# Within-chunk sums of a linear-recurrence mixer: multiply-and-reduce on two vector engines, or coefficient blocks sent through DRAM to the matrix engine

## The chip, the cores and the metric

The kernel runs on one core of one Trainium2 chip. The core has a matrix engine (PE in the profile; PEld is its weight load), a vector engine (DVE), an activation engine (ACT), a general engine (POOL, called G in the code) and a queue that issues transfers (SP). Each engine takes its instructions in the order in which the program lists them. The metric is device time in microseconds, as the median of several runs; lower is better.

## The reference, cut to what matters

Eight batch elements of 256 tokens by 512 features pass through a transformer layer (self attention, cross attention, MLP) and then through a layer of the RWKV kind: a time mix, which is a recurrence over tokens with 32 heads of 16 features, and a channel mix. The change concerns the recurrence:

```python
def step(s, rkvw):
    r_t, k_t, v_t, w_t = rkvw
    a = k_t[..., :, None] * v_t[..., None, :]
    out = jnp.einsum('bhi,bhij->bhj', r_t, u * a + s)
    s = a + w_t[..., :, None] * s
    return (s, out)
```

For one head, `out_t` is the sum over earlier tokens s < t of a coefficient A[t, s] times v_s, where A[t, s] is the product of r_t, the decays between s and t, and k_s, summed over the 16 features; the token itself counts with u in place of the decay.

## The kernel before

All arithmetic is float32. Projections split each operand into a high and a low float32r part and use three matmuls (lines 185 to 187). The kernel is one program, cut into stages, one call per batch element. The first layer's stages come first; the second layer's are

- `a` (layernorm, token shift, low-rank mix), `b` (projections g, k) and `e` (projections v, w, r). r, k, v and w of each batch element are written to DRAM.
- `c`: tokens are cut into 16 chunks of 16. r, k and w come back from DRAM in tiles `in` with (8 head groups x 16 chunks) on the 128 partitions, so that a partition holds 16 tokens of 4 heads. POOL multiplies pairs of r and k (lines 713, 714, 724, 737), DVE reduces each product over 16 features into the coefficient tile `A` (715, 730, 743), and POOL multiplies decays into r, k and w in place, doubling the reach each round (747, 748, 749). Then, for t = 0 to 15, POOL multiplies the coefficients of token t by v of tokens 0 to t (755) and DVE sums over the source tokens (762) into `ob`. The decayed k and r, the chunk decays and `ob` are stored to DRAM (`ks`, `r0`, `dd`, `on`).
- `d`: the part that crosses chunks. Small matmuls of 32x32 (807) make the contribution of each chunk to the state, a scan on DVE runs over chunks (824), small matmuls (834) apply r to the states, and their masked sums are added to `o`, which was loaded from `on` (819). A normalisation ends it, and `o` goes to DRAM as `yg`.
- `f` and `g`: the channel mix, `front` and `back`.

The order of the work is decided at build time. `SEQ` lists in which order the stages are emitted, `AT` gives each stage a priority (1000 times batch index plus offset; lower goes first), and a scheduler then fixes the order of the instructions on each engine from these priorities and its own estimates. `SLOTS` names for each tile the buffers that it takes turns in; `BANKS` does so for PSUM. `wtp` is one bank, `up` two, and `staged` tiles take turns in two buffers.

`n_tile` loads 128 tokens by 512 features from a DRAM tile that is stored by head groups; `pm` is a mask over partitions: columns 2 and 3 are one where the partition's 16-token chunk within a pair is the even or the odd one.

Of the kernel before, what the change touches and what calls it, by code (L numbers as in the profile page):

```python
# [9 lines left out]
AF = mybir.ActivationFunctionType  # L10
ALU = mybir.AluOpType
AX = mybir.AxisListType
# [5 lines left out]
P = 128  # L18
D = 512
# [20 lines left out]
def slots(text):  # L40

    r = {}
    for item in text.split():
# [15 lines left out]
    "mlp": slots("w:a8-a11 x:a0,a1 xr:a2 y:a3 u:a4-a7 hf:a12,a13 hid:a16-a23 row:b8"),  # L59
    "time": slots(  # L60
        "w:a24,a25 x:a0 xs:a4-a7 y:a3 s:a8-a11 m2h:d0 m2g:a14,a15 n:b0,b1 d2:b9 m1:d1 xn:d2 xa:d3,a13 xb:d5 "
        "in:a16-a19 ob:a12 vm:a20,a21 r0t:a22 sts:a23 on_:a2 "
        "ks:b2,b3 X:a24,a25 A:a1 sq:b8 cm:c2 gr:c3 dts:c6 s0t:c7"
    ),
    "chan": slots(
# [3 lines left out]


SEQ = (
    "a0 b0 a1 e0 c0 b1 a2 e1 c1 d0 b2 a3 e2 c2 d1 b3 a4 e3 c3 d2 b4 a5 e4 c4 d3 b5 a6 e5 c5 d4 b6 a7 e6 c6 d5 b7 "
    "e7 c7 f0 d6 f1 g0 d7 f2 g1 f3 g2 f4 g3 f5 g4 f6 g5 f7 g6 g7"
)

BANKS = {
# [5 lines left out]

AT = {"a": -0.5, "b": -8.75, "e": 1.8, "c": -9.5, "d": -9.3, "f": 6.25, "g": 7.75}
PACE = 1000

def r32(ap):
# [4 lines left out]
def block_kernel(ctx: ExitStack, tc: tile.TileContext, a: dict, out: bass.AP):  # L93
    nc = tc.nc
# [34 lines left out]
    def wt(name, shape, dt=F32):  # L129
        tag = name  # L130
        if name in SLOTS[phase[0]]:
            tags = SLOTS[phase[0]][name]
            i = turn.get((phase[0], name), 0)
            turn[phase[0], name] = i + 1
            tag = tags[i % len(tags)]
        return wk.tile(shape, dt, name=name, tag=tag)
# [162 lines left out]
    def dtile(name, shape):  # L299
        return dram.tile(shape, F32, name=name)  # L300
# [235 lines left out]
    def staged(shape):  # L536
        return wst.tile(shape, F32, name="w")

    class TimeMix:
# [148 lines left out]
        def c(self, b, got):  # L688

            rd, kd, vd, wd = got  # L690

            def from_dram(src):
                d_ = wt("in", [P, 16, 64])
                nc.sync.dma_start(out=d_, in_=src.rearrange("e (c t) d -> (e c) t d", t=16))
                return d_

            kb, rb, wb = (from_dram(z) for z in (kd, rd, wd))

            vt = wt("in", [P, 64, 16])
            for h in range(2):  # L700
                vh = staged([P, 8, 64])
                nc.sync.dma_start(out=vh, in_=vd.rearrange("e (c t) d -> (e c) t d", t=16)[:, 8 * h : 8 * h + 8, :])
                S.copy(vt[:, :, 8 * h : 8 * h + 8].rearrange("p d s -> p s d"), vh)


            A = wt("A", [P, 16, 16, 4])

            def part(t, s_, dims):
                return bass.AP(A.tensor, A.offset + 64 * t + 4 * s_, [A.ap[0], *dims])

            X = wt("X", [P, 1024])
            X3 = X.rearrange("p (t d) -> p t d", t=16)
            G.tensor_tensor(X3, rb, kb, ALU.mult)
            G.tensor_tensor(X3, X3, W["ubc"].unsqueeze(1).broadcast_to([P, 16, 64]), ALU.mult)
            V.tensor_reduce(part(0, 0, [[68, 16], [1, 4]]), X.rearrange("p (t g i) -> p t g i", t=16, i=16), AX.X, ALU.add)


            for m in (1, 2, 4, 8):
                nb = 8 // m
                R, K, Wd = (z.rearrange("p (n u) d -> p n u d", n=nb) for z in (rb, kb, wb))  # L720
                if m < 4:
                    for i in range(m):
                        X = wt("X", [P, 1024])[:, 0:512]
                        G.tensor_tensor(
                            X.rearrange("p (n s d) -> p n s d", n=nb, s=m),
                            R[:, :, m + i : m + i + 1, :].broadcast_to([P, nb, m, 64]),
                            K[:, :, 0:m, :],
                            ALU.mult,
                        )
                        V.tensor_reduce(part(m + i, 0, [[136 * m, nb], [1, 4 * m]]), X.rearrange("p (n g i) -> p n g i", n=nb, i=16), AX.X, ALU.add)  # L730
                else:
                    ni = 16 // m
                    for n in range(nb):
                        for i in range(0, m, ni):
                            t0, s0 = (2 * n + 1) * m + i, 2 * n * m
                            X = wt("X", [P, 1024])
                            G.tensor_tensor(
                                X.rearrange("p (i s d) -> p i s d", i=ni, s=m),
                                rb[:, t0 : t0 + ni, :].unsqueeze(2).broadcast_to([P, ni, m, 64]),
                                kb[:, s0 : s0 + m, :].unsqueeze(1).broadcast_to([P, ni, m, 64]),  # L740
                                ALU.mult,
                            )
                            V.tensor_reduce(part(t0, s0, [[64, ni], [1, 4 * m]]), X.rearrange("p (n g i) -> p n g i", n=ni, i=16), AX.X, ALU.add)

                wl_ = Wd[:, :, m - 1 : m, :]
                wr_ = Wd[:, :, 2 * m - 1 : 2 * m, :]
                G.tensor_tensor(R[:, :, m:, :], R[:, :, m:, :], wl_.broadcast_to([P, nb, m, 64]), ALU.mult)
                G.tensor_tensor(K[:, :, :m, :], K[:, :, :m, :], wr_.broadcast_to([P, nb, m, 64]), ALU.mult)
                G.tensor_tensor(wr_, wr_, wl_, ALU.mult)

            ob = wt("ob", [P, 16, 64])
            for t in range(16):
                n = t + 1
                Y = wt("X", [P, 1024])[:, : 64 * n] if t else ob[:, 0, :]
                G.tensor_tensor(  # L755
                    Y.rearrange("p (h j s) -> p h j s", h=4, j=16),
                    A[:, t, 0:n, :].rearrange("p s h -> p h s").unsqueeze(2).broadcast_to([P, 4, 16, n]),
                    vt[:, :, 0:n].rearrange("p (h j) s -> p h j s", j=16),
                    ALU.mult,
                )  # L760
                if t:
                    V.tensor_reduce(ob[:, t, :], Y.rearrange("p (d s) -> p d s", s=n), AX.X, ALU.add)  # L762

            def back(src, name):
                dst = dtile(f"{name}_{b}", [8, T, 64])
                nc.sync.dma_start(out=dst.rearrange("e (c t) d -> (e c) t d", t=16), in_=src)
                return dst

            dd = dtile(f"dd_{b}", [8, 16, 64])
            nc.sync.dma_start(out=dd.rearrange("e c d -> (e c) d"), in_=wb[:, 15, :])  # L770
            return back(kb, "ks"), back(rb, "r0"), dd, vd, back(ob, "on")

        def d(self, b, got):

            ksd, r0d, dd, vd, ond = got
            dn = staged([16, D])
            nc.sync.dma_start(out=dn.rearrange("c (e d) -> c e d", e=8), in_=dd.rearrange("e c d -> c e d"))
            dt_ps = bank("wtp", [P, KC, 16])
# [8 lines left out]
            centred(s0t.rearrange("p g j -> p (g j)"), KC, bank("wtp", [P, KC]))  # L787
            ks = [self.n_tile(ksd, t, "ks") for t in range(2)]

            vms = []  # L790
            for t in range(2):
                vms.append(wt("vm", [P, 2, D]))
                vn = self.n_tile(vd, t)
                for par in range(2):
                    S.activation(vms[t][:, par, :], vn, AF.Copy, scale=pm[:, 2 + par : 3 + par])

            sts = wt("sts", [P, KC, 32, 16])
            for hp in range(2):
# [15 lines left out]
            r0 = [self.n_tile(r0d, t) for t in range(2)]  # L814
            r0t = wt("r0t", [P, KC, T])
            to_t(r0, lambda k2, tp: S.copy(r0t[:, 2 * k2 : 2 * k2 + 2, :], tp), "wtp")
            o = wt("on_", [P, 2, D])
            for t in range(2):
                nc.sync.dma_start(out=o[:, t, :].rearrange("p (e d) -> p e d", e=8), in_=ond[:, t * P : (t + 1) * P, :].rearrange("e p d -> p e d"))
            for g in range(KC):  # L820
                dT = bank("up", [P, 32, 16])
                S.copy(dT, dts[:, g, :].unsqueeze(1).broadcast_to([P, 32, 16]))
# [42 lines left out]
    class ChannelMix:  # L865
# [55 lines left out]
        def back(self, b, got):  # L921
            x4, xr, xk = got
            rr = [wt("rr", [P, D]) for t in range(2)]
            proj_n([W["fr"]], [xr], lambda t, o: S.activation(rr[t], o, AF.Tanh, scale=0.5), "o2")
            kh = wt("kk", [P, KC, T], F32R)
            kl = wt("kk", [P, KC, T], F32R)

            def emit3(ks, o):
                kf = wt("kf", [P, 2, T])
                S.activation(kf, o, AF.Relu)  # L930
                V.scalar_tensor_tensor(o, o, 0.0, kf, ALU.max, ALU.mult)
                S.copy(kh[:, ks, :], o)
                V.tensor_tensor(kl[:, ks, :], o, r32(kh[:, ks, :]), ALU.subtract)

            proj_t(W["fk"], xk, emit3, "o2", pairs=True)

            def emit4(t, o):
                V.scalar_tensor_tensor(o, rr[t], 1.0, o, ALU.add, ALU.mult)
                V.scalar_tensor_tensor(x4[:, t, :], o, 0.5, x4[:, t, :], ALU.mult, ALU.add)

            proj_n([W["fv"]], [(kh, kl)], emit4, "o2")
            nc.sync.dma_start(out=tok(out[b]), in_=x4)
# [4 lines left out]
    got = {}  # L947
# [80 lines left out]
```

## Time and profile before

| What | us |
|---|---|
| Median of 3 runs (1970.3 to 1984.28) | 1973.3 |
| The profiled execution: its span, and its time as a run | 1980.5, 1982.31 |
| PE busy | 1756.4 |
| DVE busy | 1379.7 |
| ACT busy | 1106.5 |
| POOL busy | 747.5 |
| First and last start of the product that opens `c` (713) | 1239.2, 1727.9 |
| First start of the first small matmuls of `d` (807), last start of the second ones (834) | 1322.8, 1819.0 |

Times within the span are counted from its start. A group of instructions is given by line, engine, operation and tile; the number behind x is how often it stands in the trace, then come the time in which any of them ran and the mean time of one. Matmuls overlap each other, so the mean time of one is more than the distance between two starts. The code's 1024 small matmuls of line 807 (128 for each of 8 batch elements) are 2048 records in the trace, and so are those of line 834.

### The profile page before, as it was taken

The page shows a single profiled execution, that of the slowest core. Times are in us where ns is not written, and L with a number is a line of the kernel's source. Part 1 is how long each engine was busy: PE and PEld are TensorE (multiplying, and loading weights), DVE is VectorE, ACT ScalarE, POOL GpSimd, SP SyncE. Part 2 cuts the span into 40 slices and gives each one's busy share as a digit, 9 for nine tenths or more (in the row PEclk, how much of TensorE's full clock was granted, in tenths as well). Part 3 has the DMA queues.
Part 4 walks back from the last instruction along what each step waited for, and adds up shares of the span by engine and source line. Part 5 has one row for each costly group of instructions (what it writes and reads, how often), then busy time and mean ns, then how long its engine had stood idle before and what let it go on. Part 6 is the DMA issues. An engine that isn't in the chain of part 4 may idle for free.

```text
span 1980.5 us, 38765 instructions
## 1 busy us (share of the span) xinstructions
PE 1756.4 (89%) x14576; PEld 1471.8 (74%) x14576; DVE 1379.7 (70%) x3211; ACT 1106.5 (56%) x2745; POOL 747.5 (38%) x550
## 2 busy tenths in 40 slices
PE   4999999989999998999999988888889895789877
PEld 4777777777777776799999976676777673677766
DVE  4777777776778687665654454669678788888554
ACT  3877777887778688532332334354464454355342
POOL 2111111121221221232311100898899999992000
PEclk9999999999999999999999998988898886888888
DMA  6644444656555556322311133454556476442210
GB/s 189 158 125 119 118 118 125 190 142 164 132 146 143 133 135 207 110 90 69 107 65 64 54 128 103 116 142 125 157 138 165 130 195 184 142 108 97 75 64 22
DMA packets 237170, 247.35 MB, mean 125 GB/s; under 512 B 156292, under 2 KB 159244, under 8 KB 236983
## 3 DMA queue, kind: packets, MB, share of 16 engines
q1 hardware_dynamic: 236982, 244.87, 44.7%
q8 instruction: 115, 1.88, 0.4%
q14 instruction: 73, 0.59, 0.1%
HBM read 118.71 MB, written 58.98 MB: 90 GB/s over the span
## 4 chain that ended last, share of the span: by engine, by line
PE 60%; DVE 15%; DMA 6%; ACT 6%; POOL 5%; issue 3%; SPq 3%; POOLq 0%; DVEq 0%; ACTq 0%
PE o L185 8%; PE o L186 8%; PE o L187 8%; PE mm L185 5%; PE mm L186 4%; PE mm L187 4%; PE tr L366 3%; PE out L187 3%; PE out L186 3%; PE out L185 3%; DVE e L359 3%; POOL X L755 2%; PE cx L375 2%; DVE e L357 2%; PE sc L355 2%
## 5 line engine op out<-in xcount | busy, mean ns | idle before, releaser
L362 ACT ACTIVATE e<-e,mx 128x256 f32<-128x256 f32 x512 | 256.7, 506 | 43.0 <-DVE mx L359 42.0
L357 DVE TENSOR_TENSOR e<-sc,mc 128x512 f32<-128x512 f32 x256 | 172.1, 683 | 111.8 <-PE sc L355 56.2
L227 POOL TENSOR_TENSOR u<-y,u 128x1024 fp32r<-128x1024 f32 x32 | 78.5, 2452 | 440.8 <-ACT u L226 440.6
L359 DVE CUSTOM_DVE_ANT_0 e<-e,mn 128x256 f32<-128x256 f32 x512 | 220.6, 473 | 1.0
L755 POOL TENSOR_TENSOR X<-A,in 128x128 f32<-128x128 f32 (+14 forms) x120 | 209.3, 1779 | 14.7 <-DVE ob L762 12.4
L185 PE MATMUL o<-whi,s 128*128 128x512 f32 x320 | 148.4, 464 | 49.4 <-ACT s L890 31.8
L366 PE MATMUL tr<-ident,e 128*128 128x128 f32 x1024 | 174.7, 285 | 18.0 <-ACT e L362 14.7
L185 PE MATMUL mm<-u,whi 128*128 128x256 f32 x512 | 153.7, 301 | 14.3 <-DVE s L319 7.8
L370 ACT COPY pt<-tr 128x512 f32<-128x512 f32 x256 | 147.0, 582 | 34.6 <-PE tr L366 33.9
L366 PEld LDWEIGHTS tr<-ident,e 128*128 128x128 f32 x1024 | 122.3, 144 | 49.2 <-ACT e L362 24.2
L186 PE MATMUL mm<-u,whi 128*128 128x256 f32 x512 | 147.5, 288 | 4.0 <-POOL u L227 4.0
L185 PE MATMUL o<-u,whi 128*128 128x256 f32 x512 | 144.7, 287 | 3.1 <-ACT whi L171 1.6
L187 PE MATMUL mm<-u,wlo 128*128 128x256 f32 x512 | 147.0, 287 | 0.0
L186 PE MATMUL o<-u,whi 128*128 128x256 f32 x512 | 144.0, 283 | 0.0
L187 PE MATMUL o<-u,wlo 128*128 128x256 f32 x512 | 144.0, 283 | 0.0
L186 PE MATMUL o<-wlo,s 128*128 128x512 f32 x320 | 141.4, 442 | 0.0
L293 POOL TENSOR_TENSOR xr<-xr,row 128x512 f32<-128x512 f32 x48 | 65.7, 1388 | 186.0 <-DMA xr<-in_x 81.1
L355 PE MATMUL sc<-stk 128*128 128x256 f32 x512 | 118.0, 322 | 19.3 <-DVE e L357 13.9
L187 PE MATMUL o<-whi,s 128*128 128x512 f32 x320 | 134.4, 438 | 0.6 <-DVE s L891 0.5
L507 ACT ACTIVATE hf<-o,cv 128x256 f32<-128x256 f32 x128 | 59.8, 475 | 117.8 <-PE o L187 115.0
L197 POOL TENSOR_SCALAR rstd<-mv 128x2 f32<-128x2 f32 x48 | 17.2, 357 | 281.2 <-DVE mv L195 260.5
L185 PEld LDWEIGHTS o<-whi,s 128*128 128x128 f32 x320 | 70.0, 219 | 68.8 <-ACT s L890 33.3
(324 smaller groups left out, 5296.3 us busy)
## 6 DMA issues: line engine op xcount, KB each, us to landing
stk<-s SPq DMA_DIRECT2D x512, 128.0 KB, 2.4
x<-x SPq DMA_DIRECT2D x40, 512.0 KB, 4.7
x<-xr SPq DMA_DIRECT2D x24, 512.0 KB, 3.6
xr<-x SPq DMA_DIRECT2D x16, 512.0 KB, 4.8
w<-in_w SPq DMA_DIRECT2D x16, 512.0 KB, 6.7
w<-v SPq DMA_DIRECT2D x32, 256.0 KB, 3.2
x<-in_x SPq DMA_DIRECT2D x8, 512.0 KB
xr<-in_x SPq DMA_DIRECT2D x8, 512.0 KB, 3.6
```

The source lines that it names most:

```text
L185: TE.matmul(o, ah, bh, start=first, stop=False)
L186: TE.matmul(o, ah, bl, start=False, stop=False)
L187: TE.matmul(o, al, bh, start=False, stop=last)
L227: (eng or V).tensor_tensor(lo, y, r32(hi), ALU.subtract)
L293: G.tensor_tensor(x[:, t, :], x[:, t, :], r, ALU.add)
L355: TE.matmul(sc[:, t, :], qs[hm][:, hc, t * P : (t + 1) * P], ks[hm][:, hc, :], start=True, stop=True)
L357: V.tensor_tensor(e, sc, mc, ALU.mult)
L359: V.tensor_tensor_reduce(e[:, t, :], e[:, t, :], mn[:, t, :], 1.0, 3.0e38, ALU.add, ALU.min, accum_out=mx[:, kk2, hc, t : t + 1])
L362: S.activation(pr[:, t, :], e[:, t, :], AF.Exp, bias=mx[:, kk2, hc, t : t + 1], scale=-1.0, accum_out=sums[:, kk2, hc, t : t + 1])
L366: TE.transpose(pt_ps[:, kk, t * P : (t + 1) * P], pr[:, t, kk * P : (kk + 1) * P], ident)
L370: S.copy(pt, pt_ps)
L755: G.tensor_tensor(Y.rearrange("p (h j s) -> p h j s", h=4, j=16), A[:, t, 0:n, :].rearrange("p s h -> p h s").unsqueeze(2).broadcast_to([P ...
```

## The change

The coefficient tile `A` is laid out by source token, head and target token, is made once and filled with zeros, so that coefficients with s > t stay zero. The products with v and their sums leave `c`: lines 755 and 762, the two loads of v with their transposing copies (702, 703), and the store and load of `on`. Instead `c` stores `A` to DRAM (`ad`). `d` loads it with the 128 source tokens of a half (8 chunks of 16) on the partitions (`At`), writes two masked copies into `Ax`, so that for each head a block of 32 source tokens by 32 target tokens is block diagonal (even and odd chunk), and multiplies each block by the 32 tokens' v of that head: 4 blocks for each of 32 heads and 2 halves. The sums stand in one `wtp` bank per half and are copied to `o`. In `SEQ`, `d` stands one `c` later, and its priority offset goes from -9.3 to 4.

```diff
-        "in:a16-a19 ob:a12 vm:a20,a21 r0t:a22 sts:a23 on_:a2 "
+        "in:a16-a18 At:a19 Ax:a12 vm:a20,a21 r0t:a22 sts:a23 on_:a2 "
...
-    "a0 b0 a1 e0 c0 b1 a2 e1 c1 d0 b2 a3 e2 c2 d1 b3 a4 e3 c3 d2 b4 a5 e4 c4 d3 b5 a6 e5 c5 d4 b6 a7 e6 c6 d5 b7 "
-    "e7 c7 f0 d6 f1 g0 d7 f2 g1 f3 g2 f4 g3 f5 g4 f6 g5 f7 g6 g7"
+    "a0 b0 a1 e0 c0 b1 a2 e1 c1 b2 a3 e2 c2 d0 b3 a4 e3 c3 d1 b4 a5 e4 c4 d2 b5 a6 e5 c5 d3 b6 a7 e6 c6 d4 b7 e7 c7 "
+    "f0 d5 f1 g0 d6 f2 g1 d7 f3 g2 f4 g3 f5 g4 f6 g5 f7 g6 g7"
...
-AT = {"a": -0.5, "b": -8.75, "e": 1.8, "c": -9.5, "d": -9.3, "f": 6.25, "g": 7.75}
+AT = {"a": -0.5, "b": -8.75, "e": 1.8, "c": -9.5, "d": 4, "f": 6.25, "g": 7.75}
...
-            vt = wt("in", [P, 64, 16])
-            for h in range(2):
-                vh = staged([P, 8, 64])
-                nc.sync.dma_start(out=vh, in_=vd.rearrange("e (c t) d -> (e c) t d", t=16)[:, 8 * h : 8 * h + 8, :])
-                S.copy(vt[:, :, 8 * h : 8 * h + 8].rearrange("p d s -> p s d"), vh)
-            A = wt("A", [P, 16, 16, 4])
+            if b == 0:
+                self.A = wt("A", [P, 16, 4, 16])
+                G.memset(self.A, 0.0)
+            A = self.A
...
-            ob = wt("ob", [P, 16, 64])
-            for t in range(16):
-                n = t + 1
-                Y = wt("X", [P, 1024])[:, : 64 * n] if t else ob[:, 0, :]
-                G.tensor_tensor(
-                    Y.rearrange("p (h j s) -> p h j s", h=4, j=16),
-                    A[:, t, 0:n, :].rearrange("p s h -> p h s").unsqueeze(2).broadcast_to([P, 4, 16, n]),
-                    vt[:, :, 0:n].rearrange("p (h j) s -> p h j s", j=16),
-                    ALU.mult,
-                )
-                if t:
-                    V.tensor_reduce(ob[:, t, :], Y.rearrange("p (d s) -> p d s", s=n), AX.X, ALU.add)
+            ad = dtile(f"ad_{b}", [P, 16, 64])
+            nc.sync.dma_start(out=ad, in_=A.rearrange("p s h t -> p s (h t)"))
...
-            return back(kb, "ks"), back(rb, "r0"), dd, vd, back(ob, "on")
+            return back(kb, "ks"), back(rb, "r0"), dd, vd, ad
...
+            At = wt("At", [P, 2, 8, 64])
+            for t in range(2):
+                nc.sync.dma_start(out=At[:, t], in_=ad.rearrange("(e u c) s x -> u (c s) e x", e=8, u=2)[t])
+            o = wt("on_", [P, 2, D])
             vms = []
             for t in range(2):
                 vms.append(wt("vm", [P, 2, D]))
                 vn = self.n_tile(vd, t)
+                Ax = wt("Ax", [P, 32, 2, 16])
                 for par in range(2):
                     S.activation(vms[t][:, par, :], vn, AF.Copy, scale=pm[:, 2 + par : 3 + par])
+                    S.activation(Ax[:, :, par, :], At[:, t].rearrange("p e (h t) -> p (e h) t", t=16), AF.Copy, scale=pm[:, 2 + par : 3 + par])
+                av = bank("wtp", [P, D])
+                for h in range(32):
+                    js = slice(16 * h, 16 * h + 16)
+                    for pr in range(4):
+                        rws = slice(32 * pr, 32 * pr + 32)
+                        TE.matmul(av[rws, js], Ax[rws, h].rearrange("p c t -> p (c t)"), vn[rws, js], start=True, stop=True)
+                S.copy(o[:, t, :], av)
...
-            o = wt("on_", [P, 2, D])
-            for t in range(2):
-                nc.sync.dma_start(out=o[:, t, :].rearrange("p (e d) -> p e d", e=8), in_=ond[:, t * P : (t + 1) * P, :].rearrange("e p d -> p e d"))
```

The strides of the helper `part`, which places each reduction in `A`, change with the layout. The shapes of the products and reductions that fill `A` do not.

More of the change, by code (lines that the diff above doesn't have):

```diff
@@ L697, in c @@
             kb, rb, wb = (from_dram(z) for z in (kd, rd, wd))
-            vt = wt("in", [P, 64, 16])
-            for h in range(2):
-                vh = staged([P, 8, 64])
-                nc.sync.dma_start(out=vh, in_=vd.rearrange("e (c t) d -> (e c) t d", t=16)[:, 8 * h : 8 * h + 8, :])
-                S.copy(vt[:, :, 8 * h : 8 * h + 8].rearrange("p d s -> p s d"), vh)
-            A = wt("A", [P, 16, 16, 4])
+            if b == 0:
+                self.A = wt("A", [P, 16, 4, 16])
+                G.memset(self.A, 0.0)
+            A = self.A
             def part(t, s_, dims):
-                return bass.AP(A.tensor, A.offset + 64 * t + 4 * s_, [A.ap[0], *dims])
+                return bass.AP(A.tensor, A.offset + 64 * s_ + t, [A.ap[0], *dims])
             X = wt("X", [P, 1024])
@@ L714, in c @@
             G.tensor_tensor(X3, X3, W["ubc"].unsqueeze(1).broadcast_to([P, 16, 64]), ALU.mult)
-            V.tensor_reduce(part(0, 0, [[68, 16], [1, 4]]), X.rearrange("p (t g i) -> p t g i", t=16, i=16), AX.X, ALU.add)
+            V.tensor_reduce(part(0, 0, [[65, 16], [16, 4]]), X.rearrange("p (t g i) -> p t g i", t=16, i=16), AX.X, ALU.add)
             for m in (1, 2, 4, 8):
@@ L729, in c @@
                         )
-                        V.tensor_reduce(part(m + i, 0, [[136 * m, nb], [1, 4 * m]]), X.rearrange("p (n g i) -> p n g i", n=nb, i=16), AX.X, ALU.add)
+                        V.tensor_reduce(part(m + i, 0, [[130 * m, nb], [16, 4 * m]]), X.rearrange("p (n g i) -> p n g i", n=nb, i=16), AX.X, ALU.add)
                 else:
@@ L742, in c @@
                             )
-                            V.tensor_reduce(part(t0, s0, [[64, ni], [1, 4 * m]]), X.rearrange("p (n g i) -> p n g i", n=ni, i=16), AX.X, ALU.add)
+                            V.tensor_reduce(part(t0, s0, [[1, ni], [16, 4 * m]]), X.rearrange("p (n g i) -> p n g i", n=ni, i=16), AX.X, ALU.add)
                 wl_ = Wd[:, :, m - 1 : m, :]
@@ L770, in c @@
             nc.sync.dma_start(out=dd.rearrange("e c d -> (e c) d"), in_=wb[:, 15, :])
-            return back(kb, "ks"), back(rb, "r0"), dd, vd, back(ob, "on")
+            return back(kb, "ks"), back(rb, "r0"), dd, vd, ad
         def d(self, b, got):
-            ksd, r0d, dd, vd, ond = got
+            ksd, r0d, dd, vd, ad = got
             dn = staged([16, D])
```

## The prediction, made before the changed kernel was run

> **What bounds the kernel now.** I first read the page's slices of the span, to find the stretch that the change touches, and then the busy time of each engine by stretch.
>
> ```profile
> PE   4999999989999998999999988888889895789877
> ...
> POOL 2111111121221221232311100898899999992000
> PEclk9999999999999999999999998988898886888888
> ```
>
> ```profile
> 1050.00:1150.00 100.00, 100.00 (x665) 91.75 (x664) 42.76 (x96) 32.20 (x69) 16.51 (x14) 1.00 0.22 74
> 1150.00:1239.00 89.00, 76.29 (x397) 64.09 (x396) 46.23 (x72) 35.57 (x68) 3.29 (x5) 0.91 0.38 113
> 1239.00:1819.00 580.00, 487.12 (x5977) 395.72 (x5980) 466.99 (x778) 282.18 (x620) 519.58 (x356) 0.86 0.52 145
> 1819.00:1980.50 161.50, 129.43 (x656) 106.45 (x648) 93.45 (x179) 62.54 (x120) 3.72 (x8) 0.86 0.15 51
> ```
>
> The columns of the second view are the length, then PE, PEld, DVE, ACT and POOL busy with counts, then the granted PE clock, DMA share and GB/s. In 1239 to 1819, where `c` and `d` run, POOL is busy 520 of 580 us and sets the pace; `c` takes 69.8 us each (opening products from 1239.2 to 1727.9, seven steps). PE is busy 487 us there, but at a clock of 0.86. I call busy time times clock "work": 419 us, or 0.72 of the stretch. In the last stretch POOL is idle and PE does 129.4 x 0.86 = 111 us of work in 161.5: 0.69. From 1239 to the end it is 530 us of work in 741.5, a share of 0.715. The MLP stage (1050 to 1150) shows 1.00; the start of the time mix, with POOL idle, 76.3 x 0.91 / 89 = 0.78.
>
> Next, what the removed and the comparable instructions cost, by groups from 1239 on:
>
> ```profile
> L755 POOL TENSOR_TENSOR X<-A,in 128x128 f32<-128x128 f32 (+14 forms) x120 | 209.3, 1779 | 14.7 <-DVE ob L762 12.4 <-DVE A L743 1.8
> L737 POOL TENSOR_TENSOR X<-in 128x1024 f32<-128x1024 f32 x48 | 113.4, 2382 | 9.7 <-DVE A L743 9.6
> L762 DVE TENSOR_REDUCE ob<-X 128x64 f32<-128x128 f32 (+14 forms) x120 | 89.2, 745 | 10.1 <-POOL X L755 9.7
> ...
> L643 ACT COPY n<-o 128x512 f32<-128x512 f32 x42 | 24.6, 588 | 32.1 <-PE o L187 27.2 <-DMA w<-n 3.0 <-issue 1.8
> ...
> L795 ACT ACTIVATE vm<-w,pm 128x512 f32<-128x512 f32 x32 | 21.5, 719 | 7.3 <-DMA w<-v 7.3
> ```
>
> Last, the small matmuls and what stands around them, in order of time on PE:
>
> ```profile
> 1328.80 0.40 PE L187 MATMUL o<-whi,s 128*128 128x512 f32 x1
> 1329.04 0.40 PE L185 MATMUL o<-whi,s 128*128 128x512 f32 x1
> ...
> 1329.56 0.44 PE L187 MATMUL o<-whi,s 128*128 128x512 f32 x1
> 1329.93 0.99 PE L807 MATMUL up<-vm,ks 32*32 32x64 f32 x64
> 1330.86 0.33 PE L217 MATMUL wtp<-ident,w 128*128 128x128 f32 x1
> ```
>
> ```profile
> 1342.30 3.56 PE L834 MATMUL up<-sts,r0t 32*32 32x64 f32 x128
> 1345.79 0.58 PE L185 MATMUL o<-s,whi 128*128 128x256 f32 x1
> ```
>
> 64 records of L807 take 0.93 us to the next start, 14.5 ns each; 128 of L834 take 3.49 us, 27.3 ns each.
>
> **POOL.** 128 products go: 209.3 + 2.6 us (the sixteenth, a group of its own), 212 us of 520. What is left of `c` is (113.4 + 42.1 + 41.1 + 30.5 + 23.6 + 20.0 + 20.0) / 8 = 36.3 us each (L737, 747, 748, 724, 749, 714, 713). Other POOL work in the stretch is 519.6 - 211.9 - 290.7 = 17 us, 2 each. The tail of products also covered something: behind the last update of r and k, stores of both and loads of the next r and k must pass before the next `c` opens. Before, that lay beside some 26 us of L755. Now it is bare: a store of 512 KB and a load of 512 KB, 3.4 us (the store of `on`) and 3.7 us (the load of r) to landing, up to 5.8 us each in the chain of waits; I take 10 us. So POOL could open a `c` every 49 us, and 8 of them would end near 1239 + 390 = 1629, not 1797. POOL is no longer the bound. The memset of `A` is once, of 1024 elements, at most 1 us by L724's 1.28 us for 512 products.
>
> **DVE** loses 89.2 us of 467, and its 9.7 us of waits for L755; its reductions into `A` keep their shapes (a strided write of 64 results beside 1024 inputs: nothing). **ACT** loses 16 copies of 1.1 us (17.6), gains 32 masked copies by L795's 719 ns (23.0) and 16 copies out of PSUM by L643's 588 ns (9.4): +15 us on 282 in 580, beside other work. **DMA**: two loads of v and the store of `on` go, the store of `A` comes, and two loads of 256 KB in pieces of 256 bytes replace two like them: 512 KB less for each batch element, and two issues fewer on SP. Nothing of these is on the path.
>
> **New waits.** The `At` loads wait on SP for the store of `A`; behind them stand loads of v and r0 of the same `d`. The masked copies wait on ACT for `At`, and behind them the casts that feed projections. The cover is the distance from `c` to `d`: in the built order the block sums of element b begin shortly before the w projection of b+2 (L675), and w projections are 46 to 69 us apart in the trace, so nearly two such steps lie between the projections of b and its block sums, against some 36 + 2 + 10 us for `c` and its transfers. If it fails, it costs the load and store once more, 7 us for an element; I take nothing. `av` uses the one `wtp` bank, so a half waits for the copy of the other (0.6 us, 8 times), which other matmuls in the order fill.
>
> **PE, new work.** 2048 block matmuls; as L807 and L834 show two records for one in the code, 4096 records. L807 has 64 columns, the new ones 16, both contiguous. By columns the price is 14.5 / 4 = 3.6 ns (15 us); if it does not fall with columns, 14.5 (59 us); by L834, whose moving operand is strided, 27.3 (112 us). It is nearest to L807; I take the middle of the first two, 9 ns, 37 us. The trace gives L807 14.5 ns. [...] L807 and L834 keep to one row group for 32 instructions; the new ones go to another row group with every instruction and into one bank. [...]
>
> **PE, changes of shape.** In the built order the block sums stand in 105 pieces among large matmuls, and those of 807 and 834 in 83 pieces instead of 43: PE goes between large and small 318 times instead of 86, 116 pairs more. L187 to L187's successor is 0.24 us (1328.80 to 1329.04), to the first small one 0.37: 0.13 more. The last small one starts at 1329.93 + 0.99 - 0.21 = 1330.71 (0.21: the least time of one), the next large one at 1330.86: 0.15 instead of 0.015. A pair costs 0.27 us, 31 us in all.
>
> **The sum.** Work from 1239 on: 530 + 37 + 31 = 598 us. At the old share of 0.715 that would be 836 us, worse by 95. So all hangs on how far the share rises when POOL no longer paces and DVE is at 0.65 instead of 0.81. It was 0.78 where POOL was idle but only one or two elements were under way. With more elements under way it should be higher; half of the way to the MLP's 1.00 is 0.89. I take 0.83, between them: 720 us, a span of 1959, 21.5 less than the profiled one. The median was 7.2 under that span: **1952 us**. The share that leaves the time as it was is 598 / 741.5 = 0.81, which is close.
>
> **Rivals.** (1) PE takes over as forecast, share 0.80 to 0.86: 747 to 695 us, median 1979 to 1927. For it: `e` already ran ahead of `c`, and PE's waits name DVE and ACT more than POOL. (2) PE is packed well, 0.88, and the blocks cost 9 to 3.6 ns: 680 to 655 us, median 1911 to 1886. For it: DVE's and POOL's relief shortens the very chains (mix, cast, split) that PE waits for. Against: the last stretch has 0.69 with all other engines light. (3) The price of PE's new work decides, slower: at share 0.83 the change breaks even at 615 us of work, so at (615 - 530 - 31) / 4096 = 13 ns for a record. L807's own 14.5 is beyond that (620 / 0.83: 747, median 1979, and 2027 at 0.78), and L834's gives 673 / 0.83 = 811, median 2043. For it: the row group changes every time. Small matmuls can also cost clock: behind the L834 stretch shown, PE is granted 0.50 from 1345.7 to 1349.1, and it was 1.00 before. (4) The coefficients don't come in time and PE waits for them, 7 us or more in each `d`: 8 x 7 = 56 us on (1), median 2008; or POOL's order with PE's work between keeps `c` from its 49 us. Against: the cover above.
>
> **Chances.** (1) 0.42, (2) 0.18, (3) 0.33, (4) 0.07. About 1% (1954 to 1993) is what a measurement of this kernel can tell from no change. (1) lies on both sides of it, 0.24 faster and 0.18 within; (2) is faster, (3) and (4) slower. Faster 0.42, same 0.18, slower 0.40. The range takes all from (2)'s low end to (3)'s L834 price: 1886 to 2045; (1) alone is 1927 to 1979.
>
> **What would show it.** POOL busy falls by about 212 us and `c` opens more often than every 69.8 us, with idle time for the loads of r and k; if it still opens every 65 or more, PE's order paces it, not POOL. The new line's records times their distance show 37 us or another price. The last `c` should open well before 1727.9, and the busy slices of PE show 9s to the end. It is wrong if PE's waits in `d` name the `At` load or the masked copies, or if PE's clock falls below 0.86.

## The result, and the profile after

The changed kernel takes 2046.2 us (median, 2037.5 to 2051.5) beside 1977.9 for the kernel before on the same chip: a ratio of 1.034, 95% interval 1.029 to 1.040. It is slower by a little more than the forecast allowed: 1952 was predicted, and the range ended at 2045. The profiled execution spans 2043.6 us, 63.1 more than the one of before.

The slices of the changed kernel's page answer to those shown of before:

```profile
PE   4999999999999898999999988998979967899997
...
POOL 2111111211212111322111007676364361600000
PEclk9999999999999999999999998987858757889898
```

POOL has come down as forecast, from 8s and 9s to mostly 3 to 7. PE stands at 8 or 9 but for a few slices of 6 and 7 late in the stretch, and its clock has gone down to mostly 0.5 to 0.8 where it was mostly 0.8 to 0.9. By stretches of the changed kernel (length, PE, PEld, DVE, ACT, POOL busy, PE clock, DMA share, GB/s):

```profile
1400.00:1500.00 100.00, 90.35 (x1685) 73.36 (x1687) 52.67 (x90) 44.83 (x104) 62.92 (x48) 0.76 0.46 120
1500.00:1600.00 100.00, 85.91 (x1473) 69.36 (x1462) 55.56 (x85) 44.85 (x100) 49.61 (x36) 0.71 0.40 103
1600.00:1700.00 100.00, 81.25 (x1781) 63.06 (x1780) 60.97 (x110) 35.57 (x74) 36.87 (x28) 0.69 0.54 146
1700.00:1800.00 100.00, 79.62 (x1372) 60.77 (x1371) 65.82 (x107) 51.48 (x106) 41.02 (x28) 0.77 0.48 139
```

Apart from PE and its weight loads no engine is above 66 us in 100, and PE, though busy, works at about 0.73 of its clock. Over everything from 1239 us on, before and then after:

```profile
1239.00:1980.50 741.50, 616.56 (x6625) 502.17 (x6624) 560.44 (x956) 344.71 (x740) 523.30 (x364) 0.86 0.44 124
```

```profile
1239.00:2043.60 804.60, 703.90 (x10671) 559.71 (x10669) 481.87 (x828) 359.40 (x769) 304.93 (x233) 0.81 0.40 110
```

In the prediction's terms (work is busy time times clock): before, 741.5 = 530 of work + 86 lost to the clock (busy time times what the clock lacks) + 125 idle. After, 804.6 = 570 + 134 + 101. The 63 us are some 40 more of work, 48 more of lost clock, 24 less of idle time. The view gives the clock to two digits, and a hundredth of it is 6 to 7 us here, so each of these terms is good to a few us.

The waits of PE in the changed kernel, and the group on POOL that opens `c`:

```profile
PE wtp L794 <- issue: 23.2, 13, 4.7
PE up L831 <- DVE sts L821: 19.0, 6, 7.6
PE o L185 <- ACT s L887: 10.6, 5, 5.2
...
PE up L807 <- issue: 8.1, 5, 2.5
```

```profile
L709 POOL TENSOR_TENSOR X<-in 128x1024 f32<-128x1024 f32 x7 | 16.7, 2391 | 135.5 <-DMA in<-r 95.8 <-DVE n L653 29.5 <-DMA in<-k 10.3
```

POOL now sits idle for 135.5 us ahead of `c`, mostly for r, which PE's projections make. `c` opens from 1232.7 to 1728.6, every 70.8 us on average, where it was 69.8: PE has become the pace, and it is no faster than POOL was. The steps are uneven: 57, 53 and 59 us at first, then 73, 87, 70 and 96, where before all lay between 66 and 73. And the largest sum of PE's waits is for nothing that another engine does ("issue"), ahead of the new small matmuls. In order of time, on PE:

```profile
1409.57 0.22 PE L794 MATMUL wtp<-w,Ax 32*32 32x16 f32 x4
1409.60 0.22 PE L807 MATMUL up<-vm,ks 32*32 32x64 f32 x2
1409.63 1.00 PE L794 MATMUL wtp<-w,Ax 32*32 32x16 f32 x94
1413.34 0.94 PE L794 MATMUL wtp<-w,Ax 32*32 32x16 f32 x56 [2.71 <-issue]
```

The trace's instruction queue moves blocks of 16 KB; one of them starts at 1410.79, in this gap. There are 147 such blocks, 115 before. The 4096 more records with a weight load each are 8192 instructions, so the 32 more blocks come to 64 bytes for one, and a block holds 256 of them. Of the 22 gaps of 0.25 us or more within stretches of small matmuls in this run, 19 end 2.3 to 3.0 us behind the start of such a block; of the small matmuls there that follow without a gap, 13 in 100 start at such a distance. That fits PE using up small instructions faster than they come, 31 us in all (23.2 + 8.1).

### The profile page after: what moved, and what is told of

Read it like the earlier page. It is cut to its first block, busy times and chain, and to the rows that moved or that the text cites. A ratio compares the mean times of both kernels' runs of the same rounds, so it can differ in the third digit from the quotient of the medians.

```text
span 2043.6 us, 46720 instructions
## 1 busy us (share of the span) xinstructions
PE 1844.7 (90%) x18672; PEld 1531.5 (75%) x18672; DVE 1308.3 (64%) x3091; ACT 1120.8 (55%) x2777; POOL 534.9 (26%) x423
## 4 chain that ended last, share of the span: by engine, by line
PE 68%; DVE 12%; DMA 5%; POOL 5%; issue 4%; ACT 4%; SPq 2%; DVEq 0%; POOLq 0%; ACTq 0%
PE o L185 9%; PE o L187 9%; PE o L186 8%; PE mm L185 5%; PE mm L186 4%; PE mm L187 4%; PE tr L366 3%; PE out L187 3%; PE out L185 3%; PE out L186 3%; DVE e L359 3%; PE up L831 2%; PE cx L375 2%; DVE e L357 2%; PE sc L355 2%
## 5 line engine op out<-in xcount | busy, mean ns | idle before, releaser
L507 ACT ACTIVATE hf<-o,cv 128x256 f32<-128x256 f32 x128 | 59.6, 474 | 117.6 <-PE o L187 114.9
L355 PEld LDWEIGHTS sc<-stk 128*128 128x128 f32 x512 | 83.3, 200 | 43.9 <-DVE e L357 25.5
L733 POOL TENSOR_TENSOR X<-in 128x1024 f32<-128x1024 f32 x48 | 113.7, 2395 | 5.0 <-DVE A L739 5.0
L185 PEld LDWEIGHTS mm<-u,whi 128*128 128x128 f32 x512 | 99.0, 194 | 19.4 <-DVE s L319 8.6
```

The costliest lines, as they stand in the source:

```text
L185: TE.matmul(o, ah, bh, start=first, stop=False)
L355: TE.matmul(sc[:, t, :], qs[hm][:, hc, t * P : (t + 1) * P], ks[hm][:, hc, :], start=True, stop=True)
L507: S.activation(hf[:, oc, :], o, AF.Gelu_apprx_tanh, bias=c("b1", self.half * 8 + u * 4 + oc))
L733: G.tensor_tensor(X.rearrange("p (i s d) -> p i s d", i=ni, s=m), rb[:, t0 : t0 + ni, :].unsqueeze(2).broadcast_to([P, ni, m, 64]), kb[:, ...
```

## The experiments

Four theories stand against each other: the blocks' own time; the clock and the fetching that go with many small matmuls; the new order; and POOL never having been the bound that it seemed. All times are medians of 4 to 10 runs, each ratio is to the kernel before on the same chip, and the accounts below count from 1239 us, as above.

**The block sums replaced by one large matmul for each half.**

```diff
-                for h in range(32):
-                    js = slice(16 * h, 16 * h + 16)
-                    for pr in range(4):
...
+                TE.matmul(av, Ax[:, 0:4].rearrange("p h c t -> p (h c t)"), vn, start=True, stop=True)
```

> The changed kernel with the 128 block matmuls of each half replaced by one 128x128 matmul over 512 columns, so the sums with v are left out, while the coefficient store, load and masked copies stay. Theory (small blocks cost their own time, about 44 us of records, and beyond it the clock, which is granted at half after stretches of small matmuls, 40 us more than before, and 23 us of gaps while instructions are fetched): 2046 - 107 + 14 for the 16 large ones, so 1940 to 1965. Rival (order: d later and at lower priority, cut into pieces, is what costs; the blocks cost their own time alone): about 2046 - 44 + 14 = 2016, with half-clock time still near 300 us.

Measured: 1956.2 us, ratio 0.987 (0.984 to 0.990). The sums with v are missing from this kernel's result.

```profile
1239.00:1955.50 716.50, 638.13 (x6603) 490.43 (x6601) 475.82 (x828) 355.22 (x768) 304.99 (x233) 0.89 0.44 123
```

568 of work, 70 lost to the clock, 78 idle. The theory's range held. Against the changed kernel, 88 us of span go: 63 of lost clock and 22 of idle time, while busy time times clock hardly differs. An estimated 14 us of large matmuls have come in for the blocks (L217 takes 0.109 us from start to start for 128 columns in float32; 16 matmuls of 512 columns, two records each), and small matmuls slow down less at half clock than this measure assumes: in the changed kernel a block's record takes 9.0 ns from start to start at full clock and 14.4 at half, one of L831 24 and 26. `c` opens every 59.6 us here. The blocks cost more than twice the 37 us of their records, and most of what comes on top is lost clock.

**The old order in the changed kernel**: `SEQ` and `AT` of the kernel before.

```diff
...
-AT = {"a": -0.5, "b": -8.75, "e": 1.8, "c": -9.5, "d": 4, "f": 6.25, "g": 7.75}
+AT = {"a": -0.5, "b": -8.75, "e": 1.8, "c": -9.5, "d": -9.3, "f": 6.25, "g": 7.75}
```

> The changed kernel with the emission order and the priority offset of d from the kernel before; nothing else. On PE the block sums then stand in 16 pieces, not 105, and PE goes between small and large 70 times, not 318. Theory (the small blocks themselves, whatever their place, bring the clock down): 2020 to 2070, half-clock time after 1239 us still 260 us or more. Rival (order and pieces cost): 1990 or less, half-clock time back near 212 us.

Measured: 2087.9 us, ratio 1.055 (1.052 to 1.058): slower than both expected. The clock is granted at half for 328 us after 1239, so that part of the theory held. PE's waits in it:

```profile
PE wtp L794 <- issue: 56.8, 22, 4.8
PE o L185 <- ACT s L887: 31.5, 6, 5.6
PE o L185 <- ACT s L632: 20.4, 9, 5.8
PE up L807 <- issue: 19.5, 11, 4.6
```

PE goes between small and large 70 times instead of 318, yet its idle time is 180 us, not 101: waits at "issue" in small stretches go from 31 to 76 us, and the waits for ACT's casts grow. It fits that the pieces, which the prediction priced at 0.27 us a pair, also give instructions time to arrive; this run moves `d` as well, so it does not show that by itself. The order is not what makes the change slow; it saves some 40 us of it.

**The new order in the kernel before.** The same two lines the other way round.

> The kernel before with the new emission order and the new priority offset of d; nothing else. Theory (blocks): 1965 to 1995; 84 changes between small and large more than before, 42 pairs of 0.27 us, are 11 us at most. Rival (order): slower than the kernel before by 30 us or more, 2008 or more.

Measured: 1995.4 us, ratio 1.008 (1.005 to 1.011). The blocks' theory held, at the end of its range; the order costs the kernel before 17 us. It has 84 changes more on PE, 42 pairs, and some 10 us more work (540).

**The kernel before without the products with v and their sums.**

```diff
-            for t in range(16):
-                n = t + 1
...
+            G.memset(ob, 0.0)
```

> The kernel before with the products with v and their sums left out (the result tile is filled with zeros instead), everything else, order and loads included. It shows what taking 212 us from POOL and 89 us from DVE is worth by itself. If POOL paces the stretch, as the prediction had it: 1905 or less, with c opening every 55 us or less. If PE's own chains and its clock pace it as much as POOL does: 1940 to 1970, with PE idle and half-clock time little changed.

Measured: 1948.0 us, ratio 0.983 (0.979 to 0.988), and

```profile
1239.00:1941.00 702.00, 594.44 (x6581) 484.08 (x6579) 482.57 (x832) 342.89 (x736) 308.03 (x236) 0.89 0.45 124
```

212 us of POOL and 89 of DVE are worth 31 us. `c` opens every 59.6 us instead of 69.8, neither the 55 of the first theory nor as before: POOL did pace the stretch, but the next limit stands 10 us behind it: before it opens `c`, POOL now waits mostly for r (75.6 us), which PE's projections make. The work is the same (529), and its share of the time rises from 0.715 to 0.754, not to 0.83. This is about the ceiling for any way of moving the sums, as long as the order and the other small matmuls stay as they are.

**The block sums held in one piece for each half** (22 pieces instead of 105).

```diff
...
+                last = block(31, 3)
+                with tc.high_priority(8000), tc.issue_after(last.ins):
+                    for h, pr in blocks[:-1]:
+                        block(h, pr)
```

> The changed kernel with the 128 block sums of a half held together: 22 pieces in PE's order instead of 105, 258 changes between small and large instead of 318. Theory (a stretch of small matmuls uses up instructions faster than they are fetched, and counts as little activity for the clock): gaps inside small stretches grow from 31 us to 50 or more, half-clock time does not fall, 2055 to 2090. Rival (changes between small and large cost 0.27 us a pair, as predicted): 30 pairs fewer, 8 us, so 2030 to 2045 and gaps as before.

Measured: 2043.7 us, ratio 1.030 (1.027 to 1.033), not to be told from the changed kernel's. The time lies in the rival's range, but neither account of it held: waits at "issue" in small stretches went from 31 to 36 us, where the theory had 50 or more and the rival no change, and the lost clock fell from 134 to 110, while idle time rose from 101 to 111. It is inconclusive; what was saved in one term went in part into others.

**Large matmuls put between the blocks.**

```diff
+                    if h % 8 == 0:
+                        for _ in range(4):
+                            TE.matmul(av[:, 16 * h : 16 * h + 128], identr, identr, start=True, stop=True)
```

> The changed kernel with four large matmuls (128x128, 128 columns, float32r, identity on identity) into the same bank ahead of every 8 heads' block sums, which then overwrite them: 256 more large matmuls of 60 to 110 ns and 144 more changes of shape. The reading is the clock and the gaps, not the time alone, since 15 to 28 us of matmuls and up to 19 us of changes are added. Theory (the small blocks count as little activity, and are fetched too slowly): half-clock time falls from 310 us (from 1150 us on) to 270 or less, gaps from 31 to 20 or less, and the time is 2030 to 2065 despite the added work. Rival (PE's idle time behind other engines brings the clock down): half-clock time stays at 300 or more and the time is 2075 or more.

Measured: 2059.6 us, ratio 1.038 (1.036 to 1.040). Waits at "issue" fell from 31 to 13 us, as the theory had it, but the half-clock time (time with the granted clock at half) from 1150 us on only from 310 to 292, where 270 was expected, and the lost clock only from 134 to 127. Four matmuls of 128 columns between the blocks did not hold the clock up here.

**One record for a block**: `Ax` and a copy of v in bfloat16.

```diff
...
-                Ax = wt("Ax", [P, 32, 2, 16])
+                vr = wt("vb", [P, D], mybir.dt.bfloat16)
+                S.copy(vr, vn)
+                Ax = wt("Ax", [P, 32, 2, 16], mybir.dt.bfloat16)
...
```

> The changed kernel with the masked coefficients and a copy of v in bfloat16 for the block sums alone, so that each block is one record, not two (2048 fewer matmuls, 4096 fewer instructions on PE with their weight loads); 16 copies of 0.6 us more on ACT. The sums are less exact. Theory (records and the instructions behind them make the cost, through clock and fetching): about half of the 90 us between this kernel and the one with a single large matmul goes, 1990 to 2010; instruction blocks fall from 147 to about 131, gaps to 15 us or less. Rival (what costs is the wait chain around the sums: copies, one bank, late d): 2030 or more.

Measured: 1969.6 us, ratio 0.993 (0.990 to 0.996), better than either expected.

```profile
1239.00:1967.80 728.80, 662.39 (x8625) 518.91 (x8624) 476.70 (x829) 365.04 (x785) 305.67 (x234) 0.86 0.44 121
```

Half the records, but 77 of the 90 us between the changed kernel and the one without blocks are gone: 93 lost to the clock instead of 134, 66 idle instead of 101, and 131 instruction blocks. `SEQ`, `AT`, the chain of waits for the coefficients and the bank are those of the changed kernel (the scheduler made 70 pieces of it, where it made 105), so these alone are not the cause. A record is cheaper here too, 7.4 ns. The cost grows faster than the number of small matmuls.

**64x64 blocks of four chunks**, half as many in float32.

```diff
...
-                    for pr in range(4):
-                        rws = slice(32 * pr, 32 * pr + 32)
...
+                        for pr in range(2):
+                            rws = slice(64 * pr, 64 * pr + 64)
...
```

> The changed kernel with 64x64 blocks of four chunks instead of 32x32 blocks of two: half as many matmuls and instructions, in float32 as before, against twice as many masked copies on ACT (128 of 256 elements, some 40 us more on ACT). Theory (number of records and instructions): 1990 to 2020, gaps 15 us or less, half-clock time 280 or less. Rival (each block costs by its weight columns, 64 instead of 32, and ACT's copies come onto the path): 2040 or more.

Measured: 2028.3 us, ratio 1.024 (1.020 to 1.028), between the two. Waits at "issue" are small, but a record takes 30 ns at full clock instead of 9 (mean of start to start), and PE waits 7.8 us for the masked copies. Half as many records at three times the price is little gain.

**All 128 rows for every block.**

```diff
-                        TE.matmul(av[rws, js], Ax[rws, h].rearrange("p c t -> p (c t)"), vn[rws, js], start=True, stop=True)
+                        TE.matmul(av[rws, js], Ax[:, h].rearrange("p c t -> p (c t)"), vn[:, js], start=True, stop=True)
```

> The changed kernel with every block sum taken over all 128 partitions instead of its own 32 (so the sums run over tokens that do not belong to them); as many matmuls, instructions, columns and pieces as before, but four times the rows of the array in use, and no change of row group from one to the next. It asks what the clock follows. Theory (a small matmul counts as little whatever its rows, since it streams 16 columns through 32 columns of the array): half-clock time stays at 280 us or more, 2030 to 2070, 8 to 10 ns for a record. Rival (the part of the array in use counts, and the change of row group costs): half-clock time 250 or less, under 7 ns for a record, 2015 or less.

Measured: 2014.9 us, ratio 1.017 (1.013 to 1.021). Its sums take in tokens that do not belong to them, so it serves as a measurement only.

```profile
1239.00:2010.60 771.60, 689.91 (x10681) 545.62 (x10679) 478.87 (x831) 359.38 (x772) 305.78 (x234) 0.86 0.42 115
```

The price of a record stayed (9.2 ns at full clock, 9.0 before), as the theory expected; the half-clock time fell from 310 to 224 us, as the rival had it. With the same number of matmuls and the same waits at "issue" (30 us), 37 us of lost clock are gone and the time falls by 31. That ties the time to the clock. The falls to half clock do become rarer. Of the steps of 3.41 us (explained below) that ran at full clock, with block sums in a fifth or more of the step and large matmuls in less than half of it, 11 of 13 were followed by half clock in the changed kernel and 3 of 10 here, with PE busy for 0.70 and 0.71 of such a step on average. In the eight runs with such steps and 32x32 blocks it was 49 of 60, with 64x64 blocks 9 of 16 (PE busy for 0.93 on average). So at about the same busy time the fall was rarer with 128 rows than with 32; but the steps are few, and this run also stays with the same rows from one matmul to the next, so rows in use and the change of row group are not told apart.

**The first two kinds of small matmul in one record, then only the block sums, then all three kinds.** They use float16 where the run above used bfloat16.

```diff
+                S.copy(ks[t], self.n_tile(ksd, t))
...
-                vms.append(wt("vm", [P, 2, D]))
+                vms.append(wt("vm", [P, 2, D], mybir.dt.float16))
...
```

> The changed kernel with the block sums in one record each, in float16, and the small matmuls that make the chunk states (line 807) in one record each as well: the masked v is written in float16, k is copied to float16 (16 copies of 0.6 us on ACT). 3072 fewer records than the changed kernel. Theory (records of small matmuls, through clock and fetching): below the version with one-record block sums alone, so 1940 to 1962, and faster than the kernel before by 1 to 2%; half-clock time 200 us or less. Rival (that version has come to the floor that ACT, DVE and the order set, and ACT has the copies more): 1965 to 1985.

> The changed kernel with the block sums alone in one record each, in float16 instead of bfloat16, which keeps three more bits of the operands. Both theories expect what bfloat16 gave, 1960 to 1980, since nothing else differs; it is the companion to the run with the state blocks on the same chip.

Measured: 1952.0 us, ratio 0.984 (0.980 to 0.988), and 1966.1 us, ratio 0.993 (0.991 to 0.995). Both as the theory had it. The third kind takes float16 for r and for what the scan writes:

```diff
...
-                V.tensor_tensor_scan(sv, dT.rearrange("p j c -> p (j c)"), sv, 0.0, ALU.mult, ALU.add)
+                V.tensor_tensor_scan(sh[:, g].rearrange("p j c -> p (j c)"), dT.rearrange("p j c -> p (j c)"), sv, 0.0, ALU.mult, ALU.add)
...
```

> The changed kernel with all three kinds of small matmuls (block sums, chunk states of line 807, states times r of line 834) in one record each, operands in float16; the scan writes its result in float16. 4096 records fewer than the changed kernel. Theory (records of small matmuls cost their time, the clock after them and fetching): another 1024 records of 25 ns go, so 1910 to 1935. Rival (the floor is ACT, DVE and the order): 1940 to 1955, no better than with the first two kinds.

Measured: 1934.4 us, ratio 0.976 (0.973 to 0.979), the best of all runs and inside the theory's range, `c` opening every 57 us:

```profile
1239.00:1934.30 695.30, 593.72 (x6606) 460.60 (x6605) 479.74 (x833) 372.48 (x805) 309.74 (x235) 0.87 0.45 127
```

But what fell against the run with two kinds is the work, from 551 to 517 us. Lost clock and idle time (77 and 102 us, beside 68 and 84 there) did not, so for this last step the theory's range held and its reason, clock and fetching, is not shown.

**The kernel before with its two kinds in one record**, products with v still on POOL.

> The kernel before with its two kinds of small matmuls in one record each, float16 as in the companion run; products with v stay on POOL. It tells whether the gain of the companion belongs to the moved sums or to the cheaper state blocks alone. Theory (with PE relieved, POOL paces the stretch, 70 us for each c, so cheaper PE work gains little): 1955 to 1980, 20 us or more above the companion. Rival (PE's clock and work pace both kernels, POOL never did): 1940 or less.

Measured: 1952.1 us, ratio 0.986 (0.984 to 0.989): between the two expectations. `c` opens every 69.2 us, so POOL's pace is as before, and still 27 us go. Of the 45 us that the best kernel gains, 27 come from cheaper state blocks, which the kernel before can have too, and 18 from the moved sums. Moving them pays here once each small matmul is one record. These versions hold the operands concerned in 16 bits where the kernel before holds 32; what that costs in exactness is not measured here.

**What precedes a fall of the clock.** The clock records of all runs are 1.0 or 0.5, in steps of 3.41 us. I counted, for eight profiled runs (before, after, and the kernels with one large matmul, one piece, old order, no products, large ones between, bfloat16), every such step from 1150 us on that ran at full clock, by the share of it in which a matmul other than the two or three small kinds ran (matmuls overlap, and a few steps change rows with how the overlap is divided):

```
share of the step in large matmuls   steps   followed by half clock
under 0.2                               90       90
0.2 to 0.5                             205      123
0.5 and more                          1113       12
```

15 of the 90 had PE busy for 0.97 or more, with small matmuls. So a step filled with these 32x32 matmuls was followed by half clock (15 of 15) as one with more idle time was (75 of 75). The seven other runs agree for all but two of some 75 steps under 0.2; both exceptions are in the run with all rows, where PE was busy for 0.78 and 0.55 of the step. At half clock (before, after, one large matmul), none of 43 steps under 0.2 and none of 30 from 0.2 to 0.5 led back to full clock, and 83 of 130 above did. Two neighbouring steps of the changed kernel, in the view of busy times:

```profile
1483.40:1486.80 3.40, 2.65 (x170) 2.22 (x169) 1.32 (x2) 1.36 (x4) 3.40 (x4) 1.00 0.33 67
1486.80:1490.20 3.40, 2.86 (x87) 2.44 (x87) 1.37 (x2) 2.02 (x5) 3.40 (x5) 0.51 0.35 79
```

The first step has 170 matmuls, 161 of them small, with PE busy for 2.65 of 3.40 us (a wait of 1.24 us for instructions begins near its end, at 1486.10), and the next step has half the clock (0.51). Being busy with 32x32 matmuls, for 0.97 of a step or more in the 15 above, was not enough to keep the clock up.

## Why the prediction was wrong

- **POOL's load and the new pace.** POOL lost 212.6 us (747.5 to 534.9), as worked out, DVE lost 71 (89 worked out) and ACT gained 14 (15). That PE takes over was right: POOL waits for r, and `c` opens no more often. The 49 us for a `c` were not reached, and the last one opened at 1728.6, not well before 1727.9.
- **The price of a block.** 9 ns for a record was forecast and 9.0 measured at full clock. One stretch in the changed kernel shows it:

```profile
1494.13 1.34 PE L794 MATMUL wtp<-w,Ax 32*32 32x16 f32 x138
```

  137 distances in 1.34 - 0.18 us (0.18: one matmul) are 8.5 ns. The change of row group with every record, which the third rival leaned on, does not show in the price of a record: 9.0 ns with four row groups and 9.2 ns with all rows.
- **The changes of shape.** 0.27 us for a pair, 31 us, was forecast. The kernel with one large matmul has 288 changes, 99 pairs more than the kernel without products, and 39 us more work, 14 of it for its large matmuls: 25 / 99 = 0.25 us. These two differ in more than the changes, but the kernel before in the new order, with 42 pairs and some 10 us of work more, gives about the same. The size was right.
- **The failing step** is "I take 0.83", the share of time in which PE works at full clock. It was 0.71 after, no better than the 0.715 of before. With all of POOL's products gone and nothing added it is 0.754, so 0.83, taken between 0.78 and half of the way to the MLP's 1.00, was too high by itself: for the sum's 598 us the relief of POOL alone would have given 598 / 0.754, 793 us, a span of 2032. The rest of the step is the clock. Beside that run the changed kernel has 41 us more of work, 68 us more lost to the clock (134, and 65 there) and 7 us less of idle time; 134 us are more than the slack of 122 us that the forecast left for idle time and lost clock together. The work itself came to 570, not 598, though both prices were right: a small matmul at half clock counts half in it but does not take twice as long (a block's record 14.4 ns, not 18), so the measure puts part of its price under lost clock; by the distances at full and half clock that explains an estimated 7 us of the 28, and the rest is open. The prediction named the clock, in the third rival and among what would make it wrong, and put no price on it. The row that had the price was shown: 0.50 right behind a stretch of L834.
- **The rivals.** The third had the sign and nearly the time (2043 by L834's price), but not the mechanism: it decided at 13 ns for a record, and 9 were slower all the same. The fourth (coefficients late) is out: PE's waits do not name the copies, and ACT waited 2.1 us for `At`. Its second half, that `c` is kept from its 49 us, did come about, through the projections behind r. That a new wait might stand in place of the old one was not foreseen for instruction fetching, 31 us.
- **The order** was taken as given. It costs the kernel before 17 us and saves the changed one some 40.

## What to carry to other kernels

When an engine paces a stretch, take its work out and run that before pricing where the work should go: here 212 us off the busiest engine were worth 31 us, and with the rest of the kernel as it stood no new home for the work could bring much more. On PE, price small matmuls by three things: their own time, the clock in the steps of 3.4 us that they fill, and the instructions they use up; here the first was 37 us, the gaps for instructions 31, and the clock more than either, and halving the records of the blocks brought the gaps to 14 us and the lost clock from 134 to 93. A share of useful time carried over from another stage is an estimate that needs its own rows: ask what lowers the clock in the stage at hand.

## What the runs showed of the hardware that was not expected

- A step of 3.41 us filled with 32x32 matmuls is followed by half clock even with PE busy for 0.97 of it or more (15 of 15 under a large share of 0.2).
- The fall is rarer when small matmuls use more of the array (or keep to one row group, which is not told apart): in steps with block sums in a fifth or more and large matmuls in under half, 49 of 60 with 32x32 blocks, 9 of 16 with 64x64, 3 of 10 with 128 rows by 32 columns.
- Stretches of small matmuls have waits that go with the fetching of instructions: gaps of up to 4.7 us, 31 us in the changed kernel and 76 us when the stretches are not broken by large matmuls.
- 32x32 matmuls of 16 columns in four row groups and one bank start 9.0 ns apart at full clock, and 7.4 ns with one record for a block; 64x64 ones 30 ns apart.
